# Where the depthwise convolution of a layer runs: VectorE in place of TensorE

## The chip, the cores and the metric

The kernel runs on one core of one Trainium2 chip. Its time is the device time of one execution in microseconds (us). The engines are named as in the profile: PE (TensorE, the matmuls) with PEld (its weight loads), DVE (VectorE), ACT (ScalarE), POOL (GpSimd) and SP (SyncE, which issues the DMAs here). L12 is line 12 of the kernel. SBUF is the on-chip memory that all engines read; PE writes its sums into PSUM.

## The reference

Four layers are applied one after the other to x (8 images of 48 x 48 pixels and 96 channels). Each adds to x a two-dimensional state space block of its group-normed input. A layer projects 96 channels to 2 x 192, sends half of them through a 3 x 3 depthwise convolution and a SiLU, and scans the result u in four directions over the 2304 pixels with 16 states per channel:

```python
xz = x @ in_proj_w
x_val, z = (xz[..., :D_INNER], xz[..., D_INNER:])
xc = jax.lax.conv_general_dilated(xc, conv_w, (1, 1), 'SAME', ..., feature_group_count=D_INNER) + conv_b
x_val = jax.nn.silu(xc)
...
decay = jnp.exp(jnp.cumsum(log_dA, axis=1))
h = decay * jnp.cumsum(dB_u / (decay + 1e-12), axis=1)
y = jnp.einsum('bldn,bln->bld', h, C_mat)
```

The four directions are summed, normed over the channels, multiplied by SiLU(z) and projected back to 96 channels. Layers 0 to 2 scan with the recurrence h = dA h + dB u; the last layer, shown above, uses the form with the cumulated decay. There the decay falls so fast that only the first 192 pixels of each direction count, and the kernel computes only these "edges"; it tests afterwards that this was so (`faded`), and has a second, full path that runs only if it was not.

## The kernel before

Images are worked in four pairs. The 192 channels of two images make three tiles of 128 partitions: tiles 0 and 1 hold 128 channels of one image each, tile 2 the other 64 channels of both. Every step of a pair comes three ways.

- **Prologue** (`prologue`, L276): loads x, norms it, projects it (L393, L402), and copies the result into a zero-bordered array `pad` of 50 x 50 (L397, L406). `convolve` (L291) then makes u. It cuts the 2304 pixels into five chunks of up to 480, and for each issues nine matmuls with diagonal 128 x 128 matrices (`ly.diag`), one per tap, onto one PSUM bank (L301); ACT moves the bank to u and adds the bias (L309). A SiLU over the whole tile follows (L313, through L259, with an activation table loaded before and after). The projections of u to the scan's B, C and dt follow (L454 and on) and go through DRAM.
- **Scan.** In the last layer a pair has 12 groups (three tiles, two orders of the pixels, two directions) of four units each, class `Edge`, 48 units a pair. A unit treats four states: ACT makes the decays da (L880) and from them rq (L887, L888), PE spreads a row of B over the partitions into b in PSUM (L893), DVE multiplies (L898, L899) and cumulates (L901), POOL makes two products with cb (L905, L906), PE adds them up in PSUM (L913). A group begins with its dt: PE, ACT, POOL (L603, L604), DVE (L607, L611 or L614), then the cumulated sum on DVE (L839) and the one-column test `faded` (L843).
- **Epilogue** (`epilogue`, L943): 16 chunks of 144 pixels, with matmuls, activations and two DVE products each (L1009, L1031).

While the units of a pair run, the epilogue of the pair before and the prologue of the next are worked in between as generators: a `yield` ends a step, and `side_step` (called from `run`) takes the next step of whichever has made less of its total (195 and 300). In the last layer ten steps are taken per unit, the prologue's from the fifth unit on; `convolve` of tile t waits with `GATED` until the units of the pair have reached tile t. When the pair's last group begins, what is left of both is issued at once:

```python
                if unit + per == all_units:
                    drain(behind.g)
                    drain(ahead.g)
```

The prologue of the last layer's pair 0 is worked while the pair before it, of layer 2, is scanned; those of pairs 1 to 3 while the last layer's pairs 0 to 2 are. The order in which all this is recorded is held for layers 0 to 2 (`keep_order`); in the last layer the language's scheduler may arrange the instructions of each engine by its own estimates. Each engine then works its own list strictly in that order.

Buffers around the change: `pad`, `pad2` and x share three buffers of the pool `tmp`, u has four, rq three (`bb`), da five, cb nine, b in PSUM two.

Of the kernel before, what the change touches and what calls it, by code (L numbers as in the profile page):

```python
# [42 lines left out]
ALU = mybir.AluOpType  # L43
# [7 lines left out]
NB, H, W, DM = 8, 48, 48, 96  # L51
# [3 lines left out]
NLAYER = 4  # L55
# [23 lines left out]
C_CONVW, C_CONVB, C_DTB, C_ALOG, C_D, C_G, C_B = 0, 9, 10, 14, 78, 82, 83  # L79
# [23 lines left out]
def ss2d_layers_kernel(ctx: ExitStack, tc: tile.TileContext, x_in, consts, weights, out):  # L103
    nc = tc.nc
# [152 lines left out]
    def silu(o, i, **kw):  # L257

        with tc.issue_after(nc.scalar.activation(o, i, AF.Silu, **kw).ins):  # L259
            nc.scalar.preload_act_table_set("natural_log_exp_and_others")  # L260

    def bank():
        return psum.tile([P, BANK], F32, name="ps", tag="ps")
# [12 lines left out]
    def prologue(l, p, short=False, first=False):  # L276
        ly = layers[l]
# [3 lines left out]
        u = [None, None, None]  # L281
# [3 lines left out]
        def padded(name):  # L285
            pad = tmp.tile([P, H + 2, W + 2], F32, name=name, tag="tmp")
            nc.gpsimd.memset(pad[:, 0 : H + 2 : H + 1, :], 0.0)
            nc.gpsimd.memset(pad[:, 1 : H + 1, 0 : W + 2 : W + 1], 0.0)
            return pad

        def convolve(pad, t):  # L291

            while place["tiles"] < t and not first:
                yield GATED
            u[t] = upool.tile([P, L], F32, name=f"u_{l}_{p}_{t}", tag="u")
            for c0, m in CHUNKS:
                r0, nr = c0 // W, m // W
                ps = bank()
                for j in range(9):
                    dy, dx = divmod(j, 3)  # L300
                    nc.tensor.matmul(  # L301
                        ps[:, :m],
                        ly.diag[:, int(t == 2), j, :],
                        pad[:, r0 + dy : r0 + dy + nr, dx : dx + W],
                        start=(j == 0),
                        stop=(j == 8),
                    )
                    yield True
                nc.scalar.activation(  # L309
                    u[t][:, c0 : c0 + m], ps[:, :m], AF.Identity, bias=ly.column(t, C_CONVB)  # L310
                )
                yield
            silu(u[t], u[t])  # L313
            yield
# [6 lines left out]
        for b in range(2):  # L321
# [65 lines left out]
            pad = padded(f"pad_{l}_{p}_{b}")  # L387
# [23 lines left out]
            if not (first and b == 1):  # L411
                yield from convolve(pad, b)
        yield from convolve(pad2, 2)


# [124 lines left out]
        if first:  # L540

            yield from x_projections((0, 0))
            yield READY
            yield from x_projections((1, 0))
            yield from convolve(pad, 1)
            yield from x_projections((0, 1), (1, 1))
        else:
            yield from x_projections((0, 0), (0, 1), (1, 0), (1, 1))
# [773 lines left out]
```

## Time and profile before

| | us |
|---|---|
| time, median of 3 runs | 21290.81 |
| lowest and highest | 21287.53, 21323.55 |
| the profiled execution's own time | 21306.41 |
| its span in the profile | 21304.6 |
| last layer, pairs 0 to 2 | 19394 to 20689 |
| last layer, pair 3 | 20689 to 21044 |
| final epilogue | 21044 to 21304 |

The profile is of one execution. Its page gives the busy time of each engine, and the answers of the trace give the same for any stretch of time, for groups of equal instructions ("busy us, mean ns of one", then the idle time of the engine just before them and what ended it), for one source line, or one by one in order of time. Busy times of PE are modelled. fp32 matmuls appear in the trace as two instructions each.

### The profile page before, as it was taken

The page shows a single profiled execution, that of the slowest core. Times are in us where ns is not written, and L with a number is a line of the kernel's source. Part 1 is how long each engine was busy: PE and PEld are TensorE (multiplying, and loading weights), DVE is VectorE, ACT ScalarE, POOL GpSimd, SP SyncE. Part 2 cuts the span into 40 slices and gives each one's busy share as a digit, 9 for nine tenths or more (in the row PEclk, how much of TensorE's full clock was granted, in tenths as well). Part 3 has the DMA queues.
Part 4 walks back from the last instruction along what each step waited for, and adds up shares of the span by engine and source line. Part 5 has one row for each costly group of instructions (what it writes and reads, how often), then busy time and mean ns, then how long its engine had stood idle before and what let it go on. Part 6 is the DMA issues. An engine that isn't in the chain of part 4 may idle for free. (4 is left out here: it accounts for less than half of the span.)

```text
span 21304.6 us, 229326 instructions
## 1 busy us (share of the span) xinstructions
PE 18651.1 (88%) x64610; PEld 9183.5 (43%) x64610; DVE 18839.5 (88%) x15938; ACT 13518.2 (63%) x23969; POOL 17988.3 (84%) x11081
## 2 busy tenths in 40 slices
PE   8988988998998998998998988988988988988886
PEld 3333443443443443443443443443443443444555
DVE  6999999999999999999999999999999999997453
ACT  5655666666666665665665666665665665666776
POOL 5989898888899899899898889889889888896442
PEclk8999999999999999999999999999999999999887
DMA  4666676676676676676676666666666666664221
GB/s 136 195 190 192 190 196 192 188 192 193 190 198 195 187 200 193 187 202 196 187 200 192 191 193 195 186 194 194 186 195 192 187 194 191 189 193 124 78 72 52
DMA packets 1707633, 3832.97 MB, mean 180 GB/s; under 512 B 238448, under 2 KB 575216, under 8 KB 1693168
## 3 DMA queue, kind: packets, MB, share of 16 engines
q1 hardware_dynamic: 1706352, 3818.21, 61.5%
q8 instruction: 521, 8.54, 0.2%
q14 instruction: 760, 6.23, 0.1%
HBM read 3665.08 MB, written 152.27 MB: 179 GB/s over the span
## 5 line engine op out<-in xcount | busy, mean ns | idle before, releaser
L804 PE MATMUL acc<-cb,cst 128*128 128x384 f32 x27648 | 10772.4, 519 | 0.0
L768 POOL TENSOR_TENSOR cb<-cb,da 128x768 f32<-128x768 f32 x5184 | 9350.0, 1813 | 1586.3 <-DVE da L759 953.8
L804 PEld LDWEIGHTS acc<-cb,cst 128*128 128x128 f32 x27648 | 5031.9, 197 | 3972.4 <-issue 1530.2
L759 DVE TENSOR_TENSOR_SCAN da<-da,carry,b 128x768 f32<-128x768 f32 x3456 | 6267.3, 1813 | 219.0 <-DVE b L755 1.4
L755 DVE TENSOR_TENSOR b<-du,b 128x768 f32<-128x768 f32 x5184 | 4910.0, 947 | 789.6 <-PE b L743 780.1
L726 ACT ACTIVATE da<-dl,a 128x768 f32<-128x768 f32 x5184 | 4770.6, 926 | 94.0 <-POOL cb L768 61.2
L743 PE MATMUL b<-brow,pick 48*128 48x512 bf16 (+3 forms) x10368 | 2660.3, 338 | 1516.2 <-DVE da L759 1184.7
L726 ACT ACTIVATE b<-dl,a 128x768 f32<-128x768 f32 x1728 | 1560.5, 903 | 2927.1 <-DVE da L759 2673.6
L768 POOL TENSOR_TENSOR cb<-cb,bb 128x768 f32<-128x768 f32 x1728 | 3133.2, 1813 | 188.1 <-issue 63.6
L698 POOL TENSOR_TENSOR bb<-bb,du 128x768 f32<-128x768 f32 x1728 | 3131.4, 1812 | 124.5 <-DMA bb<-xd 78.8
L759 DVE TENSOR_TENSOR_SCAN da<-da,b 128x768 f32<-128x768 f32 x1728 | 3029.5, 1753 | 107.4 <-DVE b L755 0.9
L743 PEld LDWEIGHTS <-pick 48*128 48x128 bf16 (+1 forms) x10368 | 667.2, 97 | 4345.3 <-DVE da L759 2285.7
L759 DVE TENSOR_TENSOR_SCAN bb<-b,carry,bb 128x768 f32<-128x768 f32 x1152 | 2069.7, 1797 | 9.1 <-ACT b L726 6.1
L301 PE MATMUL ps<-pad,diag 128*128 128x480 f32 (+1 forms) x4320 | 1995.8, 560 | 17.0 <-DVE du L611 11.5
L650 ACT COPY carry<-da 128x1 f32<-128x1 f32 x3456 | 626.9, 181 | 1068.6 <-DVE da L759 1055.7
L590 ACT ACTIVATE ps<-ps,w 128x384 f32<-128x384 f32 (+1 forms) x912 | 496.6, 545 | 1115.0 <-PE ps L585 1114.4
L301 PEld LDWEIGHTS ps<-pad,diag 128*128 128x128 f32 x4320 | 807.4, 192 | 721.1 <-issue 293.4
L603 POOL TENSOR_TENSOR lg<-lg,w 128x384 f32<-128x384 f32 (+1 forms) x912 | 891.5, 977 | 196.7 <-ACT w L601 196.6
L759 DVE TENSOR_TENSOR_SCAN bb<-b,bb 128x768 f32<-128x768 f32 x576 | 999.2, 1735 | 15.5 <-ACT b L726 11.9
L585 PE MATMUL ps<-dts,w 6*128 6x384 f32 (+5 forms) x2432 | 819.7, 522 | 182.0 <-DVE du L611 65.9
L604 POOL TENSOR_TENSOR lg<-lg,e 128x384 f32<-128x384 f32 (+1 forms) x912 | 889.3, 975 | 71.2
L798 PE MATMUL acc<-y,cst 128*128 128x384 f32 x1008 | 625.3, 751 | 275.2 <-ACT y L819 176.2
(141 smaller groups left out, 17322.1 us busy)
## 6 DMA issues: line engine op xcount, KB each, us to landing
cb<-xd SPq DMA_DIRECT2D x4736, 384.0 KB
cb<-xd SPq DMA_DIRECT2D x4736, 192.0 KB
bb<-xd SPq DMA_DIRECT2D x1152, 384.0 KB
bb<-xd SPq DMA_DIRECT2D x1152, 192.0 KB
yd<-y SPq DMA_DIRECT2D x48, 1152.0 KB
ey<-yd SPq DMA_DIRECT2D x256, 216.0 KB
brow<-xb SPq DMA_DIRECT2D x576, 72.0 KB
ex<-xs SPq DMA_DIRECT2D x256, 108.0 KB
```

The lines of the kernel that those rows point to most:

```text
L301: nc.tensor.matmul(ps[:, :m], ly.diag[:, int(t == 2), j, :], pad[:, r0 + dy : r0 + dy + nr, dx : dx + W], start=(j == 0), stop=(j == 8),)
L585: nc.tensor.matmul(o[:, :m], ly.dtw[q0 : q0 + r, k, chans], dts[q0 : q0 + r, at], start=True, stop=True,)
L603: nc.gpsimd.tensor_sub(lg, lg, w1)
L604: nc.gpsimd.tensor_add(lg, lg, e)
L650: nc.scalar.copy(*late_act.pop(0))
L698: nc.gpsimd.tensor_mul(b, b, self.du)
L726: nc.scalar.activation(da, self.dl, AF.Exp, scale=columns_of(self.l, self.t, self.ph, self.d, n))
L743: nc.tensor.matmul(b[:, z : z + zm], w, self.brow[:k, z : z + zm], start=True, stop=True)
L755: nc.vector.tensor_mul(b, self.du, b)
L759: nc.vector.tensor_tensor_scan(way(h), way(da), way(b), start, ALU.mult, ALU.add)
L768: nc.gpsimd.tensor_mul(c, c, h)
L804: nc.tensor.matmul(self.acc[:, a, : self.m // 2], ident, c[:, a, :], start=False, stop=(n == NS - 1 and not self.turns),)
```

## The change

In the last layer, for pairs 1 to 3, `convolve` computes a whole tile at a time on DVE. The first tap is a multiply with the bias added, the other eight are multiply-adds that read a shifted view of `pad` and u and write u in place. The scalar of each is a column of the layer's parameters. Each instruction is followed by a `yield`; the SiLU over the tile stays, and the chunks, the matmuls of L301 and the evictions of L309 are skipped. Pair 0 of the last layer, the other layers and the projections are as before. Line numbers below line 295 grow by 17.

```diff
             u[t] = upool.tile([P, L], F32, name=f"u_{l}_{p}_{t}", tag="u")
+            if l == NLAYER - 1 and p > 0:
+
+                v = u[t].rearrange("p (r w) -> p r w", w=W)
+                for j in range(9):
+                    dy, dx = divmod(j, 3)
+                    z = pad[:, dy : dy + H, dx : dx + W]
+                    tap = ly.column(t, C_CONVW + j)
+                    if j == 0:
+                        nc.vector.tensor_scalar(
+                            v, z, tap, ly.column(t, C_CONVB), ALU.mult, ALU.add
+                        )
+                    else:
+                        nc.vector.scalar_tensor_tensor(v, z, tap, v, ALU.mult, ALU.add)
+                    yield
+                silu(u[t], u[t])
+                yield
+                return
             for c0, m in CHUNKS:
```

## The prediction

> **What bounds the kernel now.** I read the page's busy shares first, then the same shares in stretches of time, since the change lies in the last layer alone. Over the whole span PE and DVE look equally full:
>
> ```profile
> PE 18651.1 (88%) x64610; PEld 9183.5 (43%) x64610; DVE 18839.5 (88%) x15938; ACT 13518.2 (63%) x23969; POOL 17988.3 (84%) x11081
> ```
>
> That average says nothing of the place of the change. Cut at the one-column `faded` instructions (L843, twelve to a pair), the last layer is: pairs 0 to 2 from 19394 to 20689 us, in which the prologues of pairs 1 to 3 run; pair 3, with no prologue left; and the final epilogue. Columns: PE, PEld, DVE, ACT, POOL, granted clock, DMA share, GB/s.
>
> ```profile
> 19394.00:20689.00 1295.00, 1095.88 (x5766) 752.59 (x5766) 667.60 (x1172) 1017.29 (x1891) 565.46 (x391) 0.89 0.28 78
> 20689.00:21044.00 355.00, 238.97 (x1542) 196.05 (x1542) 198.37 (x348) 280.43 (x536) 169.90 (x111) 0.80 0.25 70
> 21044.00:21304.00 260.00, 171.99 (x1102) 147.22 (x1101) 36.05 (x64) 130.10 (x214) 16.11 (x9) 0.73 0.12 32
> ```
>
> In the first stretch PE is 85% busy, ACT 79%, DVE 52%, POOL 44%. So here VectorE has half its time free. Which engine sets the pace changes inside a pair; the same view for five stretches (four of pair 1, one of pair 3):
>
> ```profile
> 20028.42:20062.73 34.31, 32.27 (x154) 19.24 (x153) 19.56 (x37) 22.92 (x46) 18.98 (x12) 1.00 0.18 50
> 20106.24:20137.54 31.30, 29.26 (x132) 16.73 (x131) 13.90 (x25) 23.44 (x46) 11.92 (x8) 1.00 0.11 28
> 20137.54:20174.76 37.22, 36.86 (x228) 26.33 (x226) 21.51 (x40) 32.99 (x60) 20.05 (x14) 1.00 0.28 77
> 20174.76:20248.88 74.12, 51.14 (x335) 39.46 (x335) 21.73 (x39) 52.25 (x95) 18.44 (x18) 0.83 0.34 97
> 20773.73:20921.74 148.01, 104.74 (x800) 86.00 (x798) 62.47 (x110) 122.99 (x220) 46.79 (x30) 0.92 0.26 76
> ```
>
> The first two hold convolution: PE is 94% busy and ACT only 67 and 75%, so PE sets the end. In the third ACT reaches 89%. The fourth is the end of the pair, where what is left of epilogue and prologue is issued at once: no engine is over 70%, a chain of short waits. The fifth is pair 3 with edges and epilogue and no convolution: ACT 83% (122.99 of 148.01). I take 83% as the pace at which ACT works here when nothing else binds. Granted clock there is 0.92, and 0.80 over pair 3, against 1.00 in the convolution; ACT keeps its 83% all the same, so I cost a cooler PE at nothing: the cover is ACT.
>
> **What goes.** Groups of instructions by line and shape, 19390 to 21060 us (columns: count | busy us, mean ns of one | idle before):
>
> ```profile
> L301 PE MATMUL ps<-pad,diag 128*128 128x480 f32 x648 | 271.8, 573 | 4.9 <-DVE eyc L1009 4.9
> L301 PE MATMUL ps<-pad,diag 128*128 128x384 f32 x162 | 54.3, 489 | 0.6 <-ACT u L309 0.5
> L309 ACT ACTIVATE u<-ps,w 128x480 f32<-128x480 f32 x36 | 23.5, 653 | 38.3 <-PE ps L301 38.2
> L309 ACT ACTIVATE u<-ps,w 128x384 f32<-128x384 f32 x9 | 5.1, 568 | 0.4 <-PE ps L301 0.2
> ```
>
> PE loses 271.8 + 54.3 = 326 us, 36 us for each of nine tiles, and falls from 85% to about 59%. That is worth only what the PE-bound stretches lose: at ACT's 83% the two shown would take 22.92 / 0.83 = 27.6 and 28.2 us, 6.7 and 3.1 us less; 10 us a pair, 30 us in all. ACT loses 45 evictions, 28.6 us, at 83% worth 34 us.
>
> The third gain is in the order. A pair has 48 units; ten side steps are issued per unit, 400 between unit 4 and unit 44, and 195 (epilogue) + 300 (prologue) are to be placed, so about 95 are drained at the end: the 74 us stretch. A tile's convolution was 5 x 10 + 1 = 51 steps and becomes 10, so three tiles give back 123 and nothing is left to drain. The listing of the changed kernel's instructions agrees: no epilogue work after the ninth of the pair's twelve groups. At 83% those 52.25 us of ACT take 63 us; 11 us a pair, 33 in all. Sum of gains: 30 + 34 + 33 = 97 us. SP issues as many DMAs as before; those of the prologue (x, the ends of the projections, their bf16 parts) move ahead of some cb loads, whose buffers are nine deep, and POOL's memsets and splits ahead of some products on a queue that is 44% busy: no cost, unless those buffers run dry.
>
> **What comes.** Eighty-one DVE instructions of 2304 elements. No row has that length; these are nearest:
>
> ```profile
> L607 DVE SCALAR_TENSOR_TENSOR ps<-ps,lg 128x192 f32<-128x192 f32 x45 | 16.4, 365 | 124.7 <-POOL lg L604 124.7
> L898 DVE TENSOR_TENSOR b<-du,b 128x768 f32<-128x768 f32 x192 | 181.4, 955 | 173.2 <-PE b L893 172.8
> L1009 DVE TENSOR_TENSOR eyc<-eyc,ps 128x432 f32<-128x432 f32 x64 | 38.4, 599 | 123.6 <-ACT ps L1007 123.4
> ```
>
> From 432 to 768 elements the time grows by 356 ns, 1.06 ns an element; 0.955 + 1536 x 0.00106 = 2.58 us. L607 (365 ns at 192, 542 ns at 384 in the earlier layers) gives 2.3 us. The dearest row is L614, which reads u by columns: 463 ns at 192, 787 at 384, hence 4.0 us. The convolution reads rows of 48 neighbours, so it is nearest to L898: 2.56 us, and 0.04 us until a dependent instruction starts (L899 at 19492.72 for 0.96, then L901 at 19493.72). Nine make 23.4 us a tile, 211 us in all.
>
> Lying beside idle DVE does not make this free, because the listing places the nine nearly back to back. Between the first and last of a tile stand, by measured durations, 5 to 7 us of other DVE work (16 us for the third tile of a pair), 289 us in nine clusters; beside them ACT has 22 to 24 us (34 for the third), 224 us in all once overlaps between neighbours are taken off. Then ACT comes to the SiLU of u, which needs the ninth product, and everything behind that SiLU waits (da, rq and the epilogue's activations); the scans behind the cluster on DVE wait too, and with them POOL's products and PE's sums.
>
> One more cost is in the trace. L839 is the only frequent DVE instruction of this layer whose two inputs both lie in SBUF, as pad and u do:
>
> ```profile
> L839 DVE TENSOR_TENSOR_SCAN dl<-ones,dl x48: 541/548/2182, 19362.0 to 21043.2; 128x192 f32<-128x192 f32 x48
> 20263.25 1.81 POOL L906 TENSOR_TENSOR cb<-cb,rq 128x768 f32<-128x768 f32 x1 [1.38 <-DVE rq L901]
> 20263.34 2.13 DVE L839 TENSOR_TENSOR_SCAN dl<-ones,dl 128x192 f32<-128x192 f32 x1
> 19454.62 0.54 DVE L839 TENSOR_TENSOR_SCAN dl<-ones,dl 128x192 f32<-128x192 f32 x1
> ```
>
> It takes 0.55 us while POOL rests, and 2.13 us when a POOL product began just before: it ends 0.41 us after POOL does. The convolution will stop for POOL in the same way, up to 1.81 us a time. In the listing 91 us of POOL work stand in the nine clusters: bounds 0 and 91 us. With these durations laid along the first cluster, about half of its POOL work falls beside DVE instructions that read PSUM; I take 5 us a tile, 45 us.
>
> The clusters then last (289 + 45) x 1.03 for starts = 343 us. ACT's 224 us would have taken 270 us at 83%. Cost: 73 us.
>
> The Trainium skill, "SBUF — State Buffer", section "Who interferes with whom", speaks against the change beyond the row: whichever of the two starts first keeps the shared port for its whole instruction, so POOL's products would also wait for 2.56 us multiply-adds. The longest L905 here took 2.07 us instead of 1.81, so the trace hardly shows that side; POOL's idle 56% would cover it, and if instead all 91 us of the listing met, the sum would turn from 24 us faster to 23 us slower. The skill's "VectorE: DVE Perf Modes", section "The perf-mode tier table", has fp32 `tensor_scalar` at twice the rate of `tensor_tensor`, which no row here shows; by it the sum would be 9 x 1.2 = 11 us lower.
>
> **The sum.** 97 - 73 = 24 us less than the profiled execution's 21306.4 us. That one was 15.6 us over the median of the runs, 21290.8; against the median I forecast 21266 us, 0.11% faster. A measurement of this kernel tells about 0.2%, 43 us, from no change.
>
> **The rivals.**
> - Faster: POOL is met hardly at all, since its products come in gaps. Clusters last 289 x 1.03 = 298 us, cost 28, gain 69: 21222 us. For: POOL is idle 56% of this stretch. Against: its products are released by the da that ACT makes during the cluster.
> - Slower, by the port: every multiply-add meets a product, 81 x 1.81 = 147 us in place of 45. Clusters 449 us, cost 179, loss 82: 21373 us. It ends over 43 us slower from about 110 us of meetings, 1.35 us per multiply-add. For: the L839 rows. Against: only about five products stand in a cluster.
> - Slower, by the rate: multiply-adds at L614's 4.0 us add 117 us, loss 97: 21388 us. Against: the inner step is one element.
> - ACT decides alone: the drain's waits only move elsewhere. Gain 97 - 33 = 64 against 73, loss 9: 21300 us.
> - That it doesn't do what it says I leave out: the listing has 81 DVE instructions more and 405 matmuls less on the path that runs, and the order up to there is unchanged.
>
> **The numbers.** Forecast 0.37 (own range 21235 to 21300); faster rival 0.28; port 0.14; rate 0.06; ACT alone 0.15. Of the forecast's range a quarter lies beyond 0.2% faster, and of the faster rival nine tenths: 0.34. Port and rate, and a little of ACT alone: 0.23 slower. The rest, 0.43, within 0.2%. The range runs from the faster rival with a little more drain won, 21200, to short of the full port case, 21350.
>
> **What will show it.** The time to 19394 us unchanged; pair 3 about as before. L304/L308 at 2.5 to 2.7 us, with some near 4.4 where a product was met; L905/L906 with maxima above 2.1 us. No 70 us end stretch; ACT idle before the SiLU of u about 9 us a tile. It is wrong if ACT's share in the clusters stays above 80% (then faster), or if multiply-adds average over 4 us (then slower).

## The result: no measurable change

The changed kernel takes 21283.34 us (median of 20 runs), the kernel before 21290.11 us (20 runs): ratio 0.9995, 95% interval 0.9989 to 1.0002. The page and the three stretches of the last layer, cut at the same one-column instructions (now L860) as for the kernel before (the first stretch begins at the second of them); columns of the stretches: PE, PEld, DVE, ACT, POOL, granted clock, DMA share, GB/s.

```profile
PE 18455.6 (87%) x63800; PEld 9110.0 (43%) x63800; DVE 19061.9 (89%) x16019; ACT 13488.4 (63%) x23922; POOL 18055.0 (85%) x11081
```

```profile
19411.00:20685.00 1274.00, 875.46 (x4916) 664.15 (x4915) 879.96 (x1241) 981.88 (x1838) 629.08 (x391) 0.78 0.27 76
20685.00:21048.00 363.00, 246.14 (x1584) 203.11 (x1583) 205.17 (x363) 285.27 (x541) 172.12 (x111) 0.80 0.27 78
21048.00:21309.00 261.00, 171.14 (x1102) 146.24 (x1101) 35.57 (x62) 129.61 (x213) 16.13 (x9) 0.74 0.12 32
```

Three things are to be seen. The work moved as written: in pairs 0 to 2 PE fell from 1096 to 875 us and DVE rose from 668 to 880. The stretch became 21 us shorter (1294.9 to 1274.2), pair 3 became 7 us longer (355.1 to 362.2). And the last layer began at 19411 us in place of 19394, though nothing in front of it was changed: over all the profiles of this study, whose first three layers are the same code in the same order, it began between 19367 and 19411 us. The whole time carries this spread; the stretches of the last layer don't, and pairs 1 and 2, the same work twice, agree within 3 us in these two kernels (430.1 and 429.4 us in the changed one). In some kernels below they are 4 to 9 us apart. So I read the experiments by the stretch "pairs 0 to 2" and give the whole time beside it. Each stretch is taken from one profiled execution, so differences below some 10 us say little.

The new instructions and POOL's products with them, by source line (duration min/median/max in ns); the last two lines are the same products in the kernel before:

```profile
L304 DVE TENSOR_SCALAR u<-pad,w x9: 1468/1476/2334, 19473.2 to 20517.2; 128x2304 f32<-128x2304 f32 x9
L308 DVE SCALAR_TENSOR_TENSOR u<-pad,w,u x72: 2586/2618/4174, 19476.1 to 20556.3; 128x2304 f32<-128x2304 f32 x72
L922 POOL TENSOR_TENSOR cb<-cb,da x192: 1796/1813/4128, 19405.3 to 21057.3; 128x768 f32<-128x768 f32 x192
L923 POOL TENSOR_TENSOR cb<-cb,rq x192: 1792/1809/4118, 19415.5 to 21067.1; 128x768 f32<-128x768 f32 x192
```

```profile
L905 POOL TENSOR_TENSOR cb<-cb,da x192: 1792/1813/2068, 19388.2 to 21053.7; 128x768 f32<-128x768 f32 x192
L906 POOL TENSOR_TENSOR cb<-cb,rq x192: 1792/1810/1827, 19398.4 to 21063.6; 128x768 f32<-128x768 f32 x192
```

A multiply-add takes 2.6 us alone and up to 4.2 us; POOL's products, which never exceeded 2.07 us before, now reach 4.1 us. Each holds the other up: without the multiply-adds (e1 below) POOL's longest product takes 2.37 us. And the three clusters of pair 1, from the first tap to the last:

```profile
19892.28:19925.40 33.12, 18.90 (x103) 14.89 (x104) 31.97 (x22) 20.41 (x42) 17.77 (x8) 0.71 0.25 67
19964.81:19995.57 30.76, 12.95 (x92) 9.60 (x91) 29.61 (x19) 24.53 (x45) 14.44 (x6) 0.77 0.18 49
20083.08:20124.99 41.91, 29.17 (x194) 23.48 (x192) 41.31 (x38) 34.44 (x57) 18.92 (x8) 0.75 0.22 56
```

DVE is full, as foreseen. ACT, which by the prediction would be busy for 224 of 343 us or 65%, is 62, 80 and 82% busy here, and 78% over all nine clusters (242 of 312 us). Behind the clusters, in the row of the SiLU over u, ACT waited 12.1 us for the multiply-adds:

```profile
L259 ACT ACTIVATE u<-u 128x2304 f32<-128x2304 f32 x9 | 19.1, 2124 | 12.4 <-DVE u L308 12.1
```

### The profile page after: what moved, and what is told of

Read it like the earlier page. It is cut to its first block, busy times and chain, and to the rows that moved or that the text cites. A ratio compares the mean times of both kernels' runs of the same rounds, so it can differ in the third digit from the quotient of the medians.

```text
span 21309.0 us, 227739 instructions
## 1 busy us (share of the span) xinstructions
PE 18455.6 (87%) x63800; PEld 9110.0 (43%) x63800; DVE 19061.9 (89%) x16019; ACT 13488.4 (63%) x23922; POOL 18055.0 (85%) x11081
## 5 line engine op out<-in xcount | busy, mean ns | idle before, releaser
L318 PE MATMUL ps<-pad,diag 128*128 128x480 f32 (+1 forms) x3510 | 1667.9, 561 | 11.9 <-DVE du L628 11.9
L318 PEld LDWEIGHTS ps<-pad,diag 128*128 128x128 f32 x3510 | 655.7, 192 | 566.6 <-issue 166.1
```

The source lines that it names most:

```text
L318: nc.tensor.matmul(ps[:, :m], ly.diag[:, int(t == 2), j, :], pad[:, r0 + dy : r0 + dy + nr, dx : dx + W], start=(j == 0), stop=(j == 8),)
```

## The experiments

**Theory and rivals.** The first theory was that of a balance: freeing PE and ACT wins some 60 us and the better order at the end of a pair another 33, and nine full clusters on DVE pay it back. Its rival was that ACT's chains set the pace and the place of the convolution is all the same. The experiments are called e1 to e12 by their order of record.

One limit holds for all of them. In the last layer the scheduler may place instructions anew for every kernel, and it did: leaving out the taps changes the order of other instructions too. At the scale of a group the order held in each pair of kernels that is compared for the price of the taps: in pair 1 the epilogue's 16 chunks fall to the same groups with nine taps and with one.

### One tap on DVE

This is e1. Eight of the nine taps are left out of the changed kernel's convolution; its steps stay.

```diff
                     if j == 0:
                         nc.vector.tensor_scalar(...)
-                    else:
-                        nc.vector.scalar_tensor_tensor(v, z, tap, v, ALU.mult, ALU.add)
                     yield
```

> The changed kernel without eight of the nine taps of the DVE convolution (the nine steps stay, so the rest is issued in the same measure). Measured on the last layer's pairs 0 to 2: 1295 us before, 1274 us changed. Theory of the balance: what the change won by freeing PE and ending the drain, it pays back in nine clusters on DVE; without the multiply-adds (221 us of DVE) the stage falls to about 1240 us, by the price that the trace of the changed kernel gives (clusters 312 us with 242 us of ACT, 292 at 83%), and to 1200 us by the 73 us of the prediction. Rival, ACT and its chains set the pace wherever the convolution is: 1265 to 1285 us.

Pairs 0 to 2: 1267.6 us; whole time 21263.22 us, ratio to before 0.9992 (0.9983 to 1.0002). The stretch, PE to POOL as above:

```profile
19369.90:20637.50 1267.60, 901.65 (x4920) 682.64 (x4919) 685.52 (x1176) 1002.68 (x1860) 568.33 (x393) 0.78 0.27 77
```

Taking 221 us of work off DVE wins 6.6 us, inside the rival's range and no more than pairs 1 and 2 of this kernel differ (426.5 and 433.1 us). Pair 3, which has no convolution in either kernel, falls by 10 us as well (362.2 to 352.3): that is the scheduler's new order, and it is as large as the price that is sought. The balance falls, on the side of its costs: the clusters are nearly free.

### One tap on PE

In e2, the same on the kernel before, from pair 1 of the last layer on; steps, banks and evictions stay.

```diff
                 for j in range(9):
-                    nc.tensor.matmul(..., start=(j == 0), stop=(j == 8))
+                    alone = l == NLAYER - 1 and p > 0
+                    if j == 0 or not alone:
+                        nc.tensor.matmul(..., start=(j == 0), stop=(j == 8 or alone))
                     yield True
```

> The kernel before without eight of the nine taps on PE in the last layer's pairs 1 to 3; steps, banks and evictions stay, so the end of each pair is drained as before. Pairs 0 to 2 took 1295 us. Theory of the balance: PE's work is worth what the PE-bound stretches lose, 30 us: about 1265 us. If PE's whole 290 us less were on the path it would be far below 1200 us. Rival, ACT sets the pace: 1285 to 1300 us.

Pairs 0 to 2: 1242.7 us; whole time 21227.48 us, 0.9973 (0.9962 to 0.9984). The stretch:

```profile
19380.80:20623.60 1242.80, 907.78 (x5046) 672.77 (x5046) 670.82 (x1173) 1019.63 (x1899) 566.20 (x391) 0.81 0.28 81
```

PE's 290 us of matmuls are worth 52 us, not 30, and both expectations are missed. So PE gives back 52 us, DVE asks for 7, and still the change wins only 21: something else in it costs.

### 13 steps per unit, convolution on PE

This is e3, an edit of the kernel before.

```diff
-            for _ in range(10 if l in short else 0 if busy else 1):
+            for _ in range(13 if l in short else 0 if busy else 1):
```

> The kernel before with 13 side steps per unit of the last layer instead of 10, convolution on PE: the drain at the end of the pair should go without the change. Pairs 0 to 2 took 1295 us. By the prediction the drain is worth 33 us: about 1262 us, and the whole kernel about 21258 us, faster than both. Rival, its waits only move into groups of edges that then run alone at 70 to 75% of ACT: 1285 to 1300 us.

Pairs 0 to 2: 1362.0 us; whole time 21381.21 us, 1.0047 (1.0030 to 1.0064). The drain is gone and the kernel is slower by 67 us in this stretch, far from both expectations. Not all of this can be laid to the drain: with the faster pace the third tile's convolution falls into one group without a chunk of the epilogue, where PE is 99% busy and ACT 55%:

```profile
20198.93:20241.49 42.56, 41.98 (x144) 21.80 (x142) 16.07 (x30) 23.55 (x44) 15.47 (x10) 1.00 0.10 26
```

The prediction's sign for this step is in doubt here; the next experiment tests it without a convolution on PE.

### 51 steps per tile, convolution on DVE

This is e4: the changed kernel, with empty steps after each multiply-add so that a tile has 51 steps as on PE.

```diff
-                    yield
+                    for _ in range(6 if j < 5 else 5):
+                        yield
```

> The changed kernel with 51 steps per tile, as the convolution on PE had, in place of 10, so that the end of the pair is drained again. Pairs 0 to 2 took 1274 us in the changed kernel. By the prediction +33 us, about 1307 us. Rival, the drain is worth nothing since the groups left alone are no better: 1265 to 1285 us; with the multiply-adds further apart in the order it may even fall a little.

Pairs 0 to 2: 1230.0 us; whole time 21220.71 us, 0.9973 (0.9960 to 0.9985). That is below every range given. With the steps as they were, the same multiply-adds make the kernel 0.27% faster than the one before. The stretch, PE to POOL as above:

```profile
19367.00:20597.00 1230.00, 876.21 (x4956) 674.37 (x4956) 884.08 (x1253) 981.52 (x1845) 683.24 (x391) 0.78 0.29 81
```

Beside the changed kernel's 1274 us PE, ACT and DVE have the same work (ACT 981.5 against 981.9, PE 876.2 against 875.5) at the same granted clock, 0.78; POOL's 54 us more are for the most part the same products lasting longer. Only the placing differs, so here the prediction's sign for the drain is plainly wrong.

### The same with one tap

This is e7: e4 without eight of the nine taps.

> e4_dve_51_steps (pairs 0 to 2: 1230 us) without eight of the nine taps; their steps stay. What is left of the price of the multiply-adds when side work is spread: theory of the fillers, DVE had idle gaps for them: 1215 to 1230 us. By the 73 us of the prediction: about 1160 us.

Pairs 0 to 2: 1216.6 us; whole time 21230.33 us in a single run. This closes a square:

| pairs 0 to 2, us | 10 steps per tile | 51 steps per tile |
|---|---|---|
| nine taps on DVE | 1274.2 | 1230.0 |
| one tap on DVE | 1267.6 | 1216.6 |

The multiply-adds cost 7 and 13 us, close to what one execution can tell; the fewer steps cost 44 us with the multiply-adds and 51 us without. So e4 did not win because its multiply-adds stand further apart.

### Fewer steps per unit

If the count of steps left over is what matters, fewer steps per unit should do in the changed kernel what 51 steps per tile did. The edit is the number in the line shown for 13 steps: 7 (e5) and 9 (e12) in the changed kernel, 8 in the kernel before (e6) and in e4 (e8).

> The changed kernel, untouched but for 7 side steps per unit of the last layer in place of 10; the multiply-adds follow each other in ten steps as in the changed kernel. Pairs 0 to 2: changed kernel 1274 us, with 51 steps per tile (e4_dve_51_steps) 1230 us. Theory of the fillers: what counts is how many groups of edges are left with no epilogue and prologue to fill their gaps; then 7 steps do what 51 steps did, 1225 to 1245 us. Rival, e4 won because its multiply-adds stand further apart: 1265 to 1285 us.

> The kernel before with 8 side steps per unit in place of 10, convolution on PE; more is drained in the pair's last group. Pairs 0 to 2: 1295 us with 10 steps, 1362 us with 13 (e3_pe_13_steps). Theory of the fillers: the drained last group grows by about 50 us, the groups before it shrink by as much or more: 1260 to 1300 us. By the prediction, where the drain costs 11 us a pair, it costs more the longer it is: 1310 to 1330 us.

> e4_dve_51_steps with 8 side steps per unit in place of 10. Pairs 0 to 2 took 1230 us with 10. If fewer steps per unit go on helping: 1205 to 1225 us, the fastest yet; if the drain of the last group now outweighs it: 1235 to 1260 us.

> The changed kernel with 9 side steps per unit in place of 10: by count 12 steps are then left for the drain, where 10 left none (28 to spare). Pairs 0 to 2 took 1274 us with 10, 1310 us with 7. If what costs is that all side work is squeezed in ahead of the pair's last groups: 1235 to 1260 us. If the number of steps left for the end is not what decides: 1265 to 1285 us.

| kernel | pairs 0 to 2, us | whole time, us | ratio to before (95%) |
|---|---|---|---|
| changed, 7 per unit | 1310.3 | 21298.74 | 1.0005 (0.9995 to 1.0014) |
| before, 8 per unit | 1322.6 | 21326.18 | single run |
| e4, 8 per unit | 1265.7 | 21262.07 | 0.9988 (0.9978 to 0.9997) |
| changed, 9 per unit | 1288.2 | 21313.64 | single run |

All four missed their theory's range, and three missed both ranges given. On PE with 8 steps the prediction's range was met, 1310 to 1330 us: a longer drain does cost more, and its last group grew from 74 to 139 us. So the count left for the end does not decide alone. One thing that differs between the kernels can be counted: the epilogue's chunks (the L1009 instructions, shifted by the edits) between two `faded` instructions. Pair 1, each group as duration in us / chunks in it:

```
before         17/0 22/0 37/1 33/2 37/1 38/1 33/2 34/1 44/2 31/1 37/1  74/4
changed        12/0 24/0 38/2 35/1 53/1 45/3 50/3 62/4 45/2 27/0 22/0  19/0
e4 (51)        17/0 21/0 40/2 37/1 25/1 35/1 34/2 30/1 36/2 29/1 38/1  74/4
changed, 7     16/0 21/0 33/1 35/1 38/1 34/1 33/1 39/3 45/1 25/0 30/1  93/6
13 on PE       25/0 14/0 47/2 43/1 47/2 42/2 52/2 59/4 54/3 43/0 22/0  15/0
```

A group with one or two chunks takes 25 to 40 us in most cases (42 to 52 with 13 steps on PE), one with three or four 39 to 74 us, one with none 12 to 27, but for the group of 43 us shown above. In the last epilogue, where little else is left, a chunk follows the one before after 13.8 us, with ACT at 50% (129.61 of 261.00): a chunk is a chain through PE, ACT and DVE, and each of the 16 makes DVE wait for ACT (171.5 us in all). By the code, where the convolution takes 51 steps, the epilogue gets few of the ten steps while it lasts; with ten steps it is passed quickly and the epilogue runs three and four chunks to a group. In the changed kernel's pair 1 this is the middle of the pair, seven groups with 16 chunks; the rows after it are nine groups of e4 with 12 chunks, about the same work for ACT:

```profile
19861.86:20188.98 327.12, 232.41 (x1453) 178.19 (x1453) 218.91 (x280) 254.41 (x454) 134.11 (x74) 0.80 0.24 68
```

```profile
19802.90:20039.87 236.97, 178.51 (x999) 137.43 (x998) 184.79 (x251) 193.77 (x365) 140.47 (x72) 0.77 0.26 75
20039.87:20107.04 67.17, 50.12 (x309) 40.76 (x309) 54.30 (x73) 57.37 (x105) 44.21 (x23) 0.78 0.31 87
```

254.4 us of ACT take 327 us, 78%, in the changed kernel; 251.1 us take 304 us, 83%, in e4, with more of DVE's and POOL's work beside them. The groups left with hardly any side work at the end of the pair are no worse than e4's drained group: their granted clock falls to 0.64, but ACT is 69% busy in the first two of them and 73% in the third, against 70% in e4's last group (the last row):

```profile
20188.98:20237.12 48.14, 31.80 (x109) 22.66 (x107) 28.88 (x50) 33.02 (x77) 32.33 (x30) 0.64 0.34 87
20237.12:20255.96 18.84, 8.30 (x36) 6.16 (x36) 15.85 (x29) 13.73 (x30) 15.36 (x10) 0.77 0.23 69
```

```profile
20107.04:20180.67 73.63, 50.82 (x329) 38.86 (x328) 24.32 (x44) 51.86 (x94) 20.19 (x19) 0.83 0.34 102
```

### The prologue later

To move side work towards the end without changing steps or pace, the next pair's prologue begins at unit 14 (e9).

```diff
-            if unit == LAG and following:
+            if unit == (14 if l in short else LAG) and following:
```

> The changed kernel (ten steps per tile, ten per unit), with the next pair's prologue begun at unit 14 of the last layer's pairs in place of unit 4. Number of steps and pace stay, the work only comes later. Pairs 0 to 2: 1274 us changed, 1230 us with 51 steps per tile. If what the changed kernel lost lies in the groups of edges left alone at the end of each pair, fewer are left alone: 1230 to 1255 us. If placing the prologue early or late is all the same: 1265 to 1285 us.

Pairs 0 to 2: 1350.6 us; whole time 21367.89 us, 1.0034 (1.0020 to 1.0048): far outside both ranges. It cannot test what it was meant for, since the epilogue still ended with the ninth group, and it brought a wait of its own. The list of PE's waits (us in total, times, longest), and the instructions behind it:

```profile
PE ps L386 <- DVE mv L383: 83.8, 3, 28.3
```

```profile
20031.32 2.59 DVE L308 SCALAR_TENSOR_TENSOR u<-pad,w,u 128x2304 f32<-128x2304 f32 x1
20033.84 0.65 DVE L379 BATCH_NORM_STATS2 st<-x 96x6 f32<-96x480 f32 x1
20034.41 2.59 DVE L308 SCALAR_TENSOR_TENSOR u<-pad,w,u 128x2304 f32<-128x2304 f32 x1
20036.93 0.55 DVE L379 BATCH_NORM_STATS2 st<-x 96x6 f32<-96x384 f32 x1
20037.40 2.60 DVE L308 SCALAR_TENSOR_TENSOR u<-pad,w,u 128x2304 f32<-128x2304 f32 x1
20039.92 0.28 DVE L383 BATCH_NORM_AGGREGATE mv<-st 96x2 f32<-96x30 f32 x1
```

```profile
20040.34 0.45 PE L386 MATMUL ps<-mv,minus_group 96*96 96x1 f32 x2 [27.73 <-DVE mv L383]
```

The statistics of the other image are threaded between the multiply-adds, and a tiny matmul that needs them stands early in PE's list: PE stands still for 28 us, once a pair, 84 us in all, about the 76 us by which this kernel is behind the changed one; that the wait is the whole loss was not tested by a run without it. This is the cost that the prediction feared of a full cluster, on another engine. In the changed kernel no wait for L383 is among PE's eleven largest.

### 11 steps, and 6 in pair 3

e10 is e4 with 11 steps per unit; e11 is the same with 6 in pair 3, where only an epilogue runs beside the edges.

```diff
-            for _ in range(10 if l in short else 0 if busy else 1):
+            for _ in range((11 if following else 6) if l in short else 0 if busy else 1):
```

> e4_dve_51_steps with 11 side steps per unit in place of 10 (8 gave 1266 us for pairs 0 to 2, 10 gave 1230 us; on PE 13 gave 1362 against 1295 us with 10). If the last group's drain is what is left to win: 1205 to 1225 us, below every kernel so far; if groups left alone already cost more than that: 1235 to 1270 us.

> e10_dve_51_11 (51 steps per tile, 11 per unit) with 6 steps per unit in the last layer's pair 3, which has only the epilogue of pair 2 beside its edges. Pair 3 took 355 us with 10 steps in the kernel before: five groups of 43 to 50 us with 16 epilogue chunks, 15 us a chunk, then groups of edges alone. Theory: there the chain of an epilogue chunk sets the pace, not ACT; spread over more groups the epilogue costs less, pair 3 falls to 325 to 345 us and pairs 0 to 2 stay at 1223 us, about 21200 us in all, the fastest. Rival, ACT's 83% sets the pace: pair 3 stays at 350 to 360 us.

With 11 steps pairs 0 to 2 take 1223.3 us; whole time 21218.31 us, 0.9965 (0.9953 to 0.9978). With 6 in pair 3: 1222.4 us, and pair 3 takes 339.9 us in place of 356.1; the end after it 266 in place of 260 us. Whole time 21223.16 us, 0.9970 (0.9959 to 0.9981): the two can't be told apart by it. The stretches lie in the ranges that the theories gave; that e11 would be the fastest is not shown. Pair 3 has the epilogue at two chunks a group here, in groups of 33 to 41 us, where the kernel before had three and four, in groups of 43 to 50:

```profile
20622.95:20962.84 339.89, 248.49 (x1542) 203.66 (x1542) 196.57 (x336) 295.62 (x547) 165.61 (x107) 0.78 0.27 75
```

ACT is 87% busy, above the 83% that I had taken for its pace: so ACT did not set the pace of pair 3 in the kernel before. That the chain of the chunks set it is argued from the theory, whose range was met. Both kernels beat the changed one and the one before.

## Why the prediction was right, and where it was wrong

The time was right: 0.11% faster was forecast, 0.03% measured by the medians, inside "no change". That is luck: the sum held since two large errors of opposite sign, the drain and the clusters, cancelled, with a smaller one on PE and ACT.

- **PE freed and evictions gone: right in kind, too small.** 30 + 34 = 64 us were forecast. From the kernel before to e4 the stretch falls by 65 us with the multiply-adds included; their 13 us taken off, by 78. The parts were not right: eight ninths of the matmuls are worth 52 us (e2), which leaves 26 us for the evictions and the last ninth, less the first tap on DVE, if the parts add up. For the matmuls I had credited only the two stretches where PE was visibly full.
- **The drain: wrong in sign.** "A tile's convolution was 51 steps and becomes 10, nothing is left to drain" came true, and "11 us a pair, 33 in all" was counted as gain. Returning to 51 steps wins 44 us with nine taps and 51 with one (e4, e7). I judged the 74 us stretch by itself, at ACT's 83%, and did not ask what happens to the groups into which its chunks go.
- **The clusters: far too dear.** 73 us were forecast, 7 (e1) or 13 (e7) measured. Their length was nearly right, 312 us for 343: the multiply-adds as forecast (2.62 us for 2.56), the first tap 1.48 us for 2.56. What failed is that ACT would fall to 65%: it did 242 us of work in them, not 224, and was 78% busy, just under the 80% named as a sign of being wrong. Of the waiting before the SiLU of u, forecast at 9 us a tile, 12.1 us stand in two places of nine. With these lengths the prediction's own formula gives 312 - 242 / 0.83 = 20 us. It charged a cluster with all the time in which ACT was below 83%, but such gaps exist without it too. Nor does ACT "keep its 83% all the same" at a cooler PE: over all of pair 3 before it is 79% (280.43 of 355.00).
- **The shared port: right, but nearly without a price.** 45 us of meetings were forecast; the 72 multiply-adds average 3.07 us in place of 2.60, 34 us. POOL's 384 products lost 53 us as well (means 1958 and 1939 ns, before 1816 and 1810). The rule of the Trainium skill, "SBUF — State Buffer", section "Who interferes with whom", that the first to start holds the port for its whole instruction, agrees on both sides. It set little of the time: leaving out the multiply-adds, and their meetings with them, saves 7 and 13 us, and e4, where they average 3.06 us and POOL is busier still (683 us), is 44 us faster. So the slower rival by the port falls, and the one by the rate with it (2.62 us, not 4.0). The faster rival, in which POOL is met hardly at all, does not hold either. The one in which the drain is worth nothing falls by e4, not by its time, which lay inside "no change" too.
- **`tensor_scalar` at twice the rate**, from the skill's "VectorE: DVE Perf Modes", section "The perf-mode tier table", is near: 1476 ns for 2304 elements beside 2618 ns for the two-tensor form used here, 1.8 times.
- **Pair 3 "about as before"** was 7 us longer, with no convolution in it. It is 355.2 us in e4 and 352.3 us in e1, which has the changed kernel's steps, so this is a matter of the scheduler's order and not of the step count alone.

Not settled: why the step counts rank as they do, and how much of each difference is the scheduler's new order. That dense epilogue chunks are what costs is argued from the counts per group and from pair 3; the trial that was to move them alone brought another wait.

## What to carry to other kernels

A rewrite that yields fewer or more steps to a hand-made interleaving is two changes: hold the number of steps and look at the arithmetic alone, then tune the pace. Price an engine's work by deleting it from the kernel: here 221 us on a half-idle VectorE cost 7 to 13 us, and 290 us on PE cost 52. Check what else moved when you delete: a scheduler may place the rest anew. A stretch in which nothing is busy is not a gain in waiting until it is known where its work goes.

## What was not expected of the hardware

POOL's two-input products and DVE's multiply-adds with both inputs in SBUF delay each other by up to nearly the length of the other's instruction (POOL to 4.13 us from 1.81, DVE to 4.17 us from 2.59), and a stage with POOL 49% and DVE 69% busy lost 7 to 13 us by the multiply-adds, with these delays included. The granted PE clock of the stretch "pairs 0 to 2" fell from 0.89 to 0.78 when the convolution left PE, and in e2 to 0.81; e2 and e4 became faster all the same.
